# Attention with spread softmax sums: where in a step VectorE adds, inverts and sends them

## The chip, the cores and the metric

The kernel runs on one core of a Trainium2 chip. The metric is the time of one execution on the device in microseconds (us); the median of nine runs of the kernel before is 2945.12 us. A core has TensorE (PE: matmuls; its weight loads are listed as PEld), VectorE (DVE), ScalarE (ACT), GpSimd (POOL) and SyncE (SP, which here only issues DMAs). Each engine works through its own queue in order and waits on semaphores for the others.

## The reference

Two layers on 4 images of 32x32 tokens with 384 channels. The change lies in the first part of the first layer, an attention of 12 heads of 32 channels per image:

```python
attn = jax.nn.softmax(jnp.einsum('bhnd,bhmd->bhnm', q, k) * scale, axis=-1)
gp = gp_w.reshape(NH, GP_NUM, HD)
gidx = jnp.argmax(jnp.einsum('bhnd,hgd->bhng', q, gp), axis=-1)
gw = jax.nn.one_hot(gidx, GP_NUM, dtype=q.dtype)
q_mean = jnp.einsum('bhng,bhnd->bhgd', gw, q) / gw.sum(axis=2)[..., None]
qmw_t = jnp.einsum('bhgd,bhnd->bhgn', q_mean, k)
_, tidx = jax.lax.top_k(qmw_t, TOPK)
...
col = mask.sum(axis=2)
final = row[..., :, None] * col[..., None, :]
attn = attn * final
attn = attn / (attn.sum(axis=2, keepdims=True) + 1e-08)
out = jnp.einsum('bhnm,bhmd->bhnd', attn, v)
out = out.transpose(0, 2, 1, 3).reshape(B, H, W, NH * HD)
return out @ proj_w.T
```

The first sum of the softmax goes over the keys m; the second normalization goes over the queries n (axis 2), per key. So each exponential is multiplied by an inverse that belongs to its query, and the sum of these products over the queries gives a factor that belongs to its key. After the attention come a mixture of four experts, and a second layer with a local attention and a feed-forward part.

## The kernel before

**Tiles.** For each of 48 heads (4 images of 12; `NHEAD`), the scores stand with the keys on the 128 partitions and the 1024 queries along the row. A head has eight such tiles of 128 keys, taken two at a time in four *pairs* (`PAIRS`, u = 0 to 3). One pair is one *step* of the loop; there are 192 steps and a few more to drain (L860 and on). All engines' work of the attention stands in the order in which this loop issues it (the schedule of these engines is written by hand).

**One step**, in the order of issue:
- `scores(u)` (L617): eight matmuls, into `ps_s`.
- with u = 0, `gather` of the head before (L656 to L660): ScalarE copies the finished sums `ps_z` to `zr`; a DMA on SyncE's queue writes them to a row in DRAM (`z_row`), and a second one reads that row back as `zz`, with eight queries on each partition.
- `exps` (L627): ScalarE takes two exponentials of 128x1024 into the tiles `e`, of which there are 15.
- `out` of the pair seven steps back (`OUT`, L635 with `ps_o`): TensorE multiplies its `e` tiles by `wv`, the values with their factors. After a head's last pair, `keep` copies `ps_o` out (L706 to L715).
- with u = 1, `spread` of the head before (below).
- work of the preparation of the next image (norm, q, k, v, groups; `prepared`, among it DMAs that fetch input tiles, L199), top-k searches (`search`, `widen`), the projection of the image before and its routing, as far as a budget per step (`PACE`) and due times allow.
- `total(u)` (L635 with `ps_z`): TensorE sums the `e` tiles over the keys by a matmul with ones.
- in the first steps one DMA of zero fills for DRAM (L80, `room<-none`).
- `share` of the pair six steps back (`SHARE`, L683 to L693): VectorE multiplies the two `e` tiles by `rz` and by `inv` and sums each row in the same pass (L686, two passes), takes the reciprocal of the sums (L691) and multiplies the values by it (L693), which gives `wv`.
- `search`, the results of the step's other matmuls (`end`), `search` again; then, with u = 1, the next head's loads of `q4` and `k4` (L604, L605: eight DMAs on SyncE's queue).

**`spread`** (L665 to L680) takes the head's sums from `zz`: VectorE adds the two halves (L668, `zall`) and takes the inverse (L670, `rr`); a DMA writes it to a row in DRAM (`r_row`, L672), and a second one reads that row onto all 128 partitions as `rz` (L674, 512 KB). After an image's last head three small operations on VectorE follow (L678 to L680).

**The numbers of the steps.** Head m has its scores in steps 4m to 4m + 3. Its sums are gathered in step 4m + 4 and spread in step 4m + 5. Its four shares stand in steps 4m + 6 to 4m + 9, and its four `out` in steps 4m + 7 to 4m + 10. So step 4m + 5, in which head m is spread, also has the last share of head m - 1, and the first share of head m, which is the first to need `rz`, comes in the step after.

**A top-k search** (`topk`) alternates between ScalarE and VectorE: ScalarE counts the entries over a bound in one pass over 1024 (L360, L367, L404), VectorE moves the bound with two operations on one column (L371, L373) or picks the last entries (L380 to L401).

Of the kernel before, what the change touches and what calls it, by code (L numbers as in the profile page):

```python
# [153 lines left out]
def attention(net, outer, router, x, x1, unsafe, qkv_wT, gpT, proj_wT, proj_w, gate_w, gate_b):  # L154
# [15 lines left out]
    NHEAD = B * NH  # L170
# [9 lines left out]
    with ExitStack() as ctx:  # L180
# [120 lines left out]
        reached, heads, projected, valued = set(), [], set(), set()  # L301
# [415 lines left out]
        def value(b, t):  # L717
            im = images[b]
            if t % 2 == 0:
                im["v"].append(big.tile([P, 2, C], FP, name="v", tag="v", bufs=4))  # L720
            cost(2.0)
            ps = psum()
            linear(
                ps[:, : C + NE], lambda k: im["xnT"][:, k, t * P : (t + 1) * P],
                lambda k: wqkv[:, k, 2 * C :],
            )
            nc.scalar.copy(im["v"][t // 2][:, t % 2, :], ps[:, :C])
            nc.scalar.copy(im["x"][:, t, :], ps[:, C : C + NE])
            if t == NB - 1:
                valued.add(b)  # L730

        def residue(b, t):
            if late:
                o = late[0].tile([P, C], FP, name="o", tag="o", bufs=2)
            else:
                o = few.tile([P, C], FP, name="o", tag="o", bufs=1)
            residues[b, t] = o
            r = b * NTOK + t * P
            nc.sync.dma_start(out=o, in_=x[r : r + P, :])

        def project(b, t):
            im = images[b]
            r = b * NTOK + t * P
            if t == 0:
                im["o"] = few.tile([P, NB, NE], FP, name="gate_o", tag="gate_o", bufs=1)
                im["mv"] = few.tile([P, NB, 2], FP, name="mv", tag="mv")
            o = residues.pop((b, t))
            cost(2.0)
            ps = psum()
            linear(  # L750
                ps[:, : C + NE], lambda k: images[b]["q"][k][:, t * P : (t + 1) * P],
                lambda k: wproj[:, k, :],
            )
            projected.add((b, t))

            def add():
                nc.vector.tensor_tensor(o, o, ps[:, :C], ALU.add)
                nc.vector.tensor_copy(im["o"][:, t, :], ps[:, C : C + NE])
                st = few.tile([P, 6], FP, name="o_st", tag="o_st")
                nc.vector.bn_stats(st, o)  # L760
                nc.vector.bn_aggr(im["mv"][:, t, :], st)
                nc.sync.dma_start(out=x1[r : r + P, :], in_=o)

            ends.append(add)
# [42 lines left out]
        def prepared():  # L807

            nonlocal spent
            for i, unit in enumerate(pending):  # L810
                if unit is not None and (unit[1] is None or unit[1]()):
                    spent += unit[0]
                    pending[i] = next(preparing[i], None)
                    return True
            return False

        def search():

            for one in list(searching):
                if next(one, 0) == 0:  # L820
                    searching.remove(one)

        def widen(step):

            nonlocal begun
            if len(searching) < 2 and begun < len(tiles) and step >= begun * TURN - 9 and ready(*tiles[begun]):
                searching.append(topk(*tiles[begun]))
                begun += 1
                next(searching[-1])

        def begin(step):
            now[0] = step
            for f in others.pop(step, []):
                f()

        def end():
            while ends:
                ends.pop(0)()
# [21 lines left out]
        for step in range(STEPS + OUT + 2):  # L860
            n, u = divmod(step, PAIRS)
            if n < NHEAD:
                heads[n].scores(u)
            if u == 0 and 0 < n <= NHEAD:
                heads[n - 1].gather()
            if n < NHEAD:
                heads[n].exps()
            if 0 <= step - OUT < STEPS:
                heads[(step - OUT) // PAIRS].out((step - OUT) % PAIRS)
                if (step - OUT) % PAIRS == PAIRS - 1:  # L870
                    heads[(step - OUT) // PAIRS].keep()
            b, i = divmod(step, PAIRS * NH)
            goal = min(goal + (RAMP if step < 12 else PACE), spent + MOST)
            if u == 1 and 0 < n <= NHEAD:
                heads[n - 1].spread()
            begin(step)
            if step < 12:
                search()
                search()
            widen(step)  # L880
            o, t = i - OUT - 2, (i - OUT - 2) // 2
            if b and 0 <= o < 2 * NB and o % 2 == 0:
                project(b - 1, t)
            if b and 0 <= o + 1 < 2 * NB and o % 2:
                residue(b - 1, t + 1)
            if b and o > 2 * NB:
                next(routing[b - 1], None)
            if b < B:
                for t in {3: [0], 4: [1, 2], 5: [3], 6: [4], 7: [5, 6], 8: [7]}.get(i, []):
                    value(b, t)  # L890
            while spent < goal and prepared():
                pass
            if n < NHEAD:
                heads[n].total(u)
            if zeros and step >= 4:
                zeros.pop(0)()
            if 0 <= step - SHARE < STEPS:
                heads[(step - SHARE) // PAIRS].share((step - SHARE) % PAIRS)
            search()
            end()  # L900
            search()
            if u == 1 and n + 1 < NHEAD:
                heads.append(Head(n + 1))
# [1191 lines left out]
def metaformer_kernel(  # L2095
# [56 lines left out]
    with ExitStack() as outer:  # L2152
        router = routing(outer)
        eng = mybir.EngineType
        with tc.manual_schedule(engines={eng.PE, eng.DVE, eng.Activation, eng.SP}):
            left = attention(
                net, outer, router, x, x1, unsafe, qkv_wT, gpT, proj_wT, proj_w, gate_w, gate_b
            )
            done = experts(net, router, x1, x2, wup, wdown, left)
# [75 lines left out]
```

## Time and profile before

| | us |
|---|---|
| median of 9 runs | 2945.12 |
| lowest and highest run | 2934.11, 2950.93 |
| the profiled execution | 2950.63 |
| its span, first to last instruction | 2948.9 |
| TensorE busy in it | 2779.2 (94%) |
| VectorE busy | 1349.0 (46%) |
| ScalarE busy | 1215.7 (41%) |
| shares' passes on VectorE, L686, 384 of 1272 ns | 474.3 |
| exponentials on ScalarE, L627, 384 of 1110 ns | 408.0 |
| additions on VectorE, L668, 48 | first at 114.3, last at 1231.7 |

The busy times count an engine's own instructions; a matmul's end is modelled, so a busy TensorE need not be one at its peak. The profile's second part gives each engine's busy share in 40 equal slices of 73.7 us, as digits in tenths (9 is 90% or more). In the timeline, a row has its start, its duration, engine, line and operation, the tile written and the tiles read, and how many instructions are merged in it; in brackets stands the idle time of the engine just before and what ended it. In the list of waits, a row has the engine and line that waited, the releaser, the sum in us, the times and the longest. "SPq" is SyncE's queue, where the DMAs are issued. A row of windows has the stretch, its length, then busy time and count of PE, PEld, DVE, ACT and POOL, the granted clock of TensorE, the DMA engines' busy share and GB/s.

### The profile page before, as it was taken

The numbers are of one execution on the slowest core, as the hardware profiler recorded it, in microseconds if no ns is written. First come the engines' busy times: TensorE is split into PE (matmuls) and PEld (weight loads), VectorE is DVE, ScalarE is ACT, GpSimd is POOL, SyncE is SP. The second block draws the span as 40 slices with busy tenths as digits, with TensorE's granted clock in tenths as the row PEclk, the third lists the DMA queues.
The fourth block names the chain that finished last, engine by engine and source line by source line (L and its number), as shares of the span: only waits on it lengthen the run. The fifth ranks groups of instructions, "written<-read, shape, count | busy, mean of one in ns | idle before, by whom it ended". The sixth has DMA issues, their size and how long they took to land. (4 is left out here: it accounts for less than half of the span.)

```text
span 2948.9 us, 36681 instructions
## 1 busy us (share of the span) xinstructions
PE 2779.2 (94%) x13236; PEld 1474.5 (50%) x13236; DVE 1349.0 (46%) x3714; ACT 1215.7 (41%) x2023; POOL 395.2 (13%) x499
## 2 busy tenths in 40 slices
PE   6989999999989997699999999999999999999988
PEld 4323333333333332167777777777777754444433
DVE  1366777776766687633000001111111147777642
ACT  3777777777767776321121121121121122122135
POOL 1000000110021003114111112212211102100000
PEclk9999999999999998799999999999999999999988
DMA  5133334222322232355445455555555437544432
GB/s 102 43 99 93 94 93 128 74 58 68 97 54 58 66 101 63 113 204 194 172 183 190 171 195 207 195 210 214 191 214 211 144 134 238 188 154 161 143 104 87
DMA packets 216991, 405.91 MB, mean 138 GB/s; under 512 B 83504, under 2 KB 177904, under 8 KB 203744
## 3 DMA queue, kind: packets, MB, share of 16 engines
q1 hardware_dynamic: 186656, 190.77, 21.7%
q0 software_dynamic: 27152, 209.66, 20.7%
q10 hardware_dynamic: 2992, 3.03, 0.3%
q8 instruction: 107, 1.75, 0.3%
q14 instruction: 84, 0.69, 0.1%
HBM read 305.35 MB, written 49.99 MB: 120 GB/s over the span
## 5 line engine op out<-in xcount | busy, mean ns | idle before, releaser
L1611 ACT ACTIVATE h<-ps_h,up 128x256 f32<-128x256 f32 x420 | 199.0, 474 | 915.2 <-PE ps_h L1607 915.1
L1607 PE MATMUL ps_h<-xbT,up 128*128 128x256 f32 x2520 | 553.1, 380 | 2.6 <-ACT h L1611 1.8
L1624 PE MATMUL ps_y<-down,h 128*128 128x384 f32 x1680 | 554.9, 487 | 0.0
L1607 PEld LDWEIGHTS ps_h<-xbT,up 128*128 128x128 f32 x2520 | 479.5, 190 | 77.8 <-ACT h L1611 2.7
L686 DVE CUSTOM_DVE_ANT_0 e<-e,rz,inv 128x1024 f32<-128x1024 f32 x384 | 474.3, 1272 | 65.2 <-DMA rz<-r_row 65.2
L627 ACT ACTIVATE e<-ps_s,shift 128x1024 f32<-128x1024 f32 x384 | 408.0, 1110 | 118.0 <-PE ps_s L617 97.5
L1624 PEld LDWEIGHTS ps_y<-down,h 128*128 128x128 f32 x1680 | 317.4, 191 | 207.2 <-issue 1.5
L1629 DVE TENSOR_TENSOR y<-ps_y,down 128x384 f32<-128x384 f32 x70 | 39.0, 557 | 720.8 <-PE ps_y L1624 720.8
L635 PE MATMUL ps_z<-e,rt_ones 128*32 128x512 f32 x1536 | 266.2, 621 | 41.4 <-ACT e L627 41.4
L635 PE MATMUL ps_o<-e,wv 128*32 128x512 f32 x1536 | 220.9, 648 | 39.2 <-DVE wv L693 29.0
L617 PE MATMUL ps_s<-q,k 32*128 32x512 f32 x1536 | 230.3, 670 | 0.0
L713 POOL DMA_DIRECT2D q<-po x96 | 76.2, 873 | 994.0 <-DMA q<-po 544.5
L367 ACT ACTIVATE below<-tk_left,tk_bound 128x1024 bf16<-128x1024 f32 (+1 forms) x160 | 184.0, 1150 | 35.7 <-DVE tk_bound L373 16.4
L1735 PE MATMUL ps_a<-wa,xnT 128*128 128x486 f32 x384 | 166.2, 581 | 7.7 <-DVE attn L1745 6.0
L617 PEld LDWEIGHTS ps_s<-q,k 32*128 32x128 f32 x1536 | 61.9, 188 | 166.5 <-issue 165.7
L282 PE MATMUL ps_t<-xnT,wqkv 128*128 128x512 f32 x288 | 137.4, 618 | 7.2 <-ACT xnT L463 5.1
L635 PEld LDWEIGHTS ps_z<-e,rt_ones 128*32 128x32 f32 x1536 | 42.6, 110 | 190.8 <-ACT e L627 115.0
L635 PEld LDWEIGHTS ps_o<-e,wv 128*32 128x32 f32 x1536 | 31.3, 111 | 198.4 <-issue 77.2
L1735 PEld LDWEIGHTS ps_a<-wa,xnT 128*128 128x128 f32 x384 | 71.3, 191 | 91.9 <-issue 84.3
L1837 PE MATMUL ps_y<-band,v 128*32 128x194 f32 (+2 forms) x960 | 102.7, 517 | 7.4 <-DMA band<-room 7.2
L1576 DVE SCALAR_TENSOR_TENSOR x<-yt,weight,x 128x384 f32<-128x384 f32 x38 | 23.5, 619 | 185.7 <-DMA x<-x 185.0
L1490 POOL DMA_INDIRECT yt<-yg,index x64 | 66.0, 1032 | 302.5 <-DVE x L1576 140.5
(342 smaller groups left out, 2860.1 us busy)
## 6 DMA issues: line engine op xcount, KB each, us to landing
band<-room SPq DMA_DIRECT2D x32, 1560.0 KB
rz<-r_row SPq DMA_DIRECT2D x48, 512.0 KB
yg<-y SPq DMA_DIRECT2D x70, 192.0 KB
q<-q SPq DMA_DIRECT2D x192, 64.0 KB
k<-k SPq DMA_DIRECT2D x192, 64.0 KB
room<-none SPq DMA_DIRECT2D x64, 192.0 KB
x<-x SPq DMA_DIRECT2D x38, 192.0 KB
o<-in_x_dram SPq DMA_DIRECT2D x33, 192.0 KB
```

The costliest lines, as they stand in the source:

```text
L282: nc.tensor.matmul(ps, lhsT=lhsT(k), rhs=rhs(k), start=k == 0, stop=k == KC - 1)
L367: nc.scalar.activation(junk[:n], left[:n], AF.Sign, bias=bound[:n], accum_out=over[:n])
L617: nc.tensor.matmul(ps[:, half * 512 : half * 512 + 512], lhsT=self.k4[r, u * P : (u + 1) * P], rhs=self.q4[r, :], start=True, stop=True,)
L627: nc.scalar.activation(e, ps, AF.Exp, bias=shift, scale=QK_SCALE)
L635: nc.tensor.matmul(ps[r : r + 32, :], lhsT=lhsT(odd), rhs=self.es[2 * u + odd][:, half * 512 : half * 512 + 512], start=u == 0, stop=u == ...
L686: nc.vector.tensor_tensor_reduce(self.es[m], self.es[m], self.rz, 1.0, self.im["inv"][:, m, self.h : self.h + 1], ALU.mult, ALU.add, self. ...
L713: nc.gpsimd.dma_start(out=there, in_=po[r : r + 32, :], accum_op=ALU.add)
L1607: nc.tensor.matmul(ps, lhsT=up[:, o : o + P], rhs=xbT[:, k, :], start=k == 0, stop=k == KC - 1,)
L1611: nc.scalar.activation(h, ps, AF.Gelu, bias=up[:, KC * HID + f : KC * HID + f + 1])
L1624: nc.tensor.matmul(ps, lhsT=hs[f][:, t * P : (t + 1) * P], rhs=down[:, f * C : (f + 1) * C], start=f == 0, stop=f == NF - 1,)
L1735: nc.tensor.matmul(pa[:, hh, :HW_], lhsT=xnT[:, k, :], rhs=wa[:, k, hh * HW_ : (hh + 1) * HW_], start=k == 0, stop=k == KC - 1,)
L1837: nc.tensor.matmul(ys[c][32 * n : 32 * n + 32, lo - 512 * half : hi - 512 * half], lhsT=vs[b, t][:, h * HD : (h + 1) * HD], rhs=bands[b, t ...
```

## The change

`spread` is called later in the step: behind the shares that the step gives VectorE, instead of ahead of the step's preparations. The function itself stays as it is, and so does everything else.

```diff
             goal = min(goal + (RAMP if step < 12 else PACE), spent + MOST)
-            if u == 1 and 0 < n <= NHEAD:
-                heads[n - 1].spread()
             begin(step)
...
             if 0 <= step - SHARE < STEPS:
                 heads[(step - SHARE) // PAIRS].share((step - SHARE) % PAIRS)
+            if u == 1 and 0 < n <= NHEAD:
+                heads[n - 1].spread()
             search()
             end()
             search()
```

On VectorE's queue, the addition and the inverse of head m move behind the last share of head m - 1, and behind whatever else of the step's preparations VectorE has. On SyncE's queue, the issues of `r_row` and `rz` move behind what the preparations and the zero fills of that step issue there.

## The prediction, made before the changed kernel ran

> **What bounds the kernel now.** I read the page's slices first, then the waits of the attention stage alone (110 to 1260 us), then the timeline head by head, SyncE's queue among it.
>
> ```profile
> span 2948.9 us, 36681 instructions
> PE   6989999999989997699999999999999999999988
> DVE  1366777776766687633000001111111147777642
> ```
>
> TensorE (PE) is busy nearly everywhere. The change touches slices 2 to 17, the attention: there TensorE sets the pace, and VectorE (DVE) is 60 to 80% busy. What follows (experts, second layer) starts when the attention ends, and a delay of TensorE in the attention is a delay of the end.
>
> ```profile
> DVE e L686 <- DMA rz<-r_row: 65.2, 31, 6.1
> DVE zall L668 <- DMA zz<-z_row: 60.2, 27, 9.4
> PE ps_o L635 <- DVE wv L693: 29.0, 13, 6.5
> SPq L199 <- ACT xn L492: 14.9, 4, 5.2
> ```
>
> (us in all, times, longest.) VectorE waits twice per head: 27 of 48 times for the sums (zz), ahead of the addition, and 31 times for the spread inverse (rz), ahead of the head's first share. TensorE waits directly for a share's product only 13 times. Head 41 in the timeline shows the chain:
>
> ```profile
> 1097.28 0.17 DVE L668 TENSOR_TENSOR zall<-zz 128x8 f32<-128x8 f32 x1
> 1097.60 1.23 DVE L686 CUSTOM_DVE_ANT_0 e<-e,rz,inv 128x1024 f32<-128x1024 f32 x1
> 1097.71 0.32 SPq L672 DMA_DIRECT2D r_row<-rr  x1
> 1099.11 0.32 SPq L674 DMA_DIRECT2D rz<-r_row  x1
> 1100.35 0.23 DVE L693 TENSOR_TENSOR wv<-v,d 128x64 f32<-128x64 f32 x1
> ...
> 1103.25 1.28 DVE L686 CUSTOM_DVE_ANT_0 e<-e,rz,inv 128x1024 f32<-128x1024 f32 x1 [1.54 <-DMA rz<-r_row]
> ...
> 1106.05 0.23 DVE L693 TENSOR_TENSOR wv<-v,d 128x64 f32<-128x64 f32 x1
> ...
> 1106.52 1.06 PE L635 MATMUL ps_o<-e,wv 128*32 128x512 f32 x8
> ```
>
> Addition 1097.28; the share of the head before it, 1097.60 to 1100.58; the inverse goes out at 1097.71, comes back by 1103.25; the own first share ends at 1106.28, and TensorE takes it 0.24 us later. Addition to first share is 6.0 us, and VectorE waits within it.
>
> **The change, part by part.** Nothing is added or removed: addition (0.17 us) and inverse (0.20) of 48 heads, with two DMA issues each, move behind one share of VectorE: two passes of 1.28, two reads of 0.08, reciprocal 0.17, product 0.23, together 3.0 us from first start to last end (2.9 to 3.06 over the heads). The order of both programs' instructions shows it for 47 heads (head 0 has no share before it, only two top-k steps of 0.15); TensorE, ScalarE and GpSimd keep theirs.
>
> *Delay of the inverse.* If VectorE waited g for the sums, the share now runs inside that wait: the addition comes d = max(0, 3.0 - g) later. In 21 heads g is under 0.15 (d = 3.0), in 19 between, in 8 (4, 5, 10, 13, 17, 23, 27, 45) at least 3, where d = 0. In a few heads small operations stand between too (heads 18 and 30: 0.6; 26: 2.5). The transfers behind it, 1.4 us to r_row's landing and 4.0 to rz's (medians), move by d. If VectorE already waited for rz (31 heads), the first share starts d later; else d less the time by which rz was early. Over 48 heads these shifts add up to 77 us.
>
> *What hides it.* TensorE needs the product only at ps_o two steps later. The slack from the end of the product to that matmul, read per head, has a median of 2.8 us. Cover lacking is the difference: heads 0 1.0, 7 0.2, 8 0.3, 11 0.3, 14 0.4, 19 2.2, 30 0.7, 38 1.5, 39 0.1, 40 2.1, 41 2.6 (2.86 against 0.24), 43 3.0 (3.1 against 0.15), and in the tail 46 0.3 and 47 1.2, where every step waits for the last: 16 us. In the other heads the whole shift is covered.
>
> *ScalarE's queue.* Its top-k passes wait for VectorE operations behind the share, and the exponentials of the next step queue behind them; TensorE's sums (ps_z) wait for these. In head 8 VectorE runs from the share at 311.04 to L400 at 322.16 without a gap, ScalarE's L404 waits 0.94 for it, and TensorE then 2.76 for an exponential: the shift of 2.9 comes through, 2 us beyond the 0.3 above. Heads 7 and 38 give 1.2 and 0.6 in the same way: 4 us in all.
>
> *SyncE's queue.* The inverse's two DMAs are moved past what the step issues otherwise: zero fills of 192 KB, which wait for nothing, and once a fetch of input tiles (L199), in head 15's step:
>
> ```profile
> 466.70 0.32 SPq L672 DMA_DIRECT2D r_row<-rr  x1
> 468.24 0.32 SPq L674 DMA_DIRECT2D rz<-r_row  x1
> 473.85 0.38 SPq L199 DMA_DIRECT2D xt<-in_x_dram  x1
> ```
>
> That fetch stands from 468.6 to 473.85 waiting for ScalarE to have read the old tile. It will now stand ahead of r_row, which can go at about 474.9 (0.4 for the fetch, 0.54 for a zero fill). Right behind such a fetch the transfers are slow; head 17 has that order now:
>
> ```profile
> 522.03 0.38 SPq L199 DMA_DIRECT2D xt<-in_x_dram  x1
> 523.11 0.56 SPq L672 DMA_DIRECT2D r_row<-rr  x1
> 527.54 0.33 SPq L674 DMA_DIRECT2D rz<-r_row  x1
> 532.00 1.28 DVE L686 CUSTOM_DVE_ANT_0 e<-e,rz,inv 128x1024 f32<-128x1024 f32 x1 [6.14 <-DMA rz<-r_row]
> ```
>
> So r_row takes 4.4 and rz 4.4 instead of 1.5 and 3.6; rz lands at 483.8, the product comes 2.95 later at 486.7, and its matmul, at 479.07 now, waits 7.6 us (with the usual 1.4 and 4.0, 4.2 us). The next head's q and k loads, eight DMAs behind rz, shift by d too; in head 21 they are issued by 625 and used after 636, which covers 3 us. A later addition also holds r_row's SyncE place longer; stores of x1 stand behind it in both orders.
>
> *Gain.* VectorE's last share no longer waits for the sums, so what follows it in the step is earlier by min(3.0, g). TensorE profits where it waits for that: head 32, whose L404 waits 1.06, so 1.1 us. In the tail TensorE waits 6.48 (head 45) and 4.53 (head 47) for this very share, but its next product waits for rz (4.95 and 1.66), which comes no sooner: nothing.
>
> *Given back.* After a stall VectorE and ScalarE have caught up, and later waits in the same step shrink (41: 1.74 at the next product; 0, 7, 14, 43 in smaller ones): 5.5 us.
>
> *Clock.* TensorE's granted clock falls after some poor stretches:
>
> ```profile
> 1110.00:1115.00 5.00, 3.00 (x16) 0.60 (x16) 4.24 (x15) 4.77 (x7) 0.06 (x1) 1.00 0.14 21
> 1120.00:1125.00 5.00, 3.25 (x12) 0.53 (x12) 4.66 (x24) 2.13 (x3) 0.00 (x0) 0.66 0.02 1
> ```
>
> (The clock is the third column from the end.) A wait of 3.56 at 1112.0 leaves it at 1.00; after one of 1.74 at 1120.2 it is 0.66 of 5 us, 1.7 us lost, and while it is low eight ps_o matmuls take 1.92 us instead of 1.07. The seven new stalls over 1.4 us (8, 15, 19, 38, 40, 41, 43) can each cost 1.7 us or nothing: 0 to 12, and I take a third, 4, since both cases stand in these rows and part of the time TensorE has no work to lose.
>
> The sum: 16 + 4 + 7.6 - 1.1 - 5.5 + 4 = 25 us, on a profiled execution of 2950.6 (span 2948.9); that is 5.5 above the runs' median of 2945.1, so 2970 for the median.
>
> Two rules of the Trainium skill, which the sum does without. "DMA: Bandwidth & Descriptors", section Rules for kernel authors, speaks against the change: issue a DMA early, compute, and wait for it late. The trace agrees where slack is small (head 41), and not where the share fits into the wait for the sums (head 5, g = 3.5); taken without exceptions it would make the whole 77 us a loss. "TensorE: Matmul & The Clock Gate", Part 1, has the clock halved after an idle window of about 3.4 us; by it only head 15's stall would count, some 1.7 us instead of my 4 and 23 instead of 25; the rows above show 0.66 after shorter waits.
>
> **The rivals.**
> - *Covered.* The shifts stay in the slack, and the fetch has passed before r_row is ready. Slack of 2.8 against shifts of at most 3.6 speaks for it; the tail (1.5) less 1.1 gives 2945 to 2948. Against: slack under 0.3 in heads 40, 41 and 43, where TensorE already waits, and the fetch's wait ends at a ScalarE instruction that the change doesn't make earlier.
> - *Faster.* The 60.2 us of waiting for sums are filled with shares, and TensorE's two waits of 6.48 and 4.53 in the tail go: 2945 - 11 = 2934. It decides if rz, not the share, is early enough by 3 us in heads 45 and 47. Against: both of their first shares wait for rz now.
> - *VectorE becomes the bound.* Waits for rz rise by 3.0 in 31 heads (93 us) and waits for sums fall by under 60; where top-k work is dense the shift doesn't fade within the head. With half of the 77 us through, and head 15: 2945 + 46 = 2991.
>
> **How the numbers follow.** Forecast (2951 to 2984) 0.60, covered 0.15, faster 0.11, VectorE bound 0.14. The range of 2946 to 2990 reaches up to the sum with nothing given back and the full clock loss (25 + 5.5 + 8 = 38.5, so 2984) and a little into the third rival, and down past the sum with the short fetch, no clock loss and twice as much given back (25 - 3.4 - 4 - 5.5 = 12, so 2957) to the covered case. 0.2% (6 us) is about what a measurement of this kernel tells from no change: faster 0.11, same 0.15, slower 0.74.
>
> **What would show it.** In the changed profile: waits of L668 for zz nearly gone (about 10 us, most of it head 45), waits of L686 for rz above 130 us; a TensorE wait of 4 to 8 us at ps_o in head 15's second step, near 480; new waits of 2 to 3 us at ps_o in heads 38 to 43; the stages after the attention unchanged. Wrong, if TensorE's idle time before 1260 us doesn't grow, or if the waits for rz stay near 65.

## The result, and the profile after

| | before | changed |
|---|---|---|
| median, us (runs) | 2942.85 (31) | 2979.58 (10) |
| lowest and highest run | 2931.59, 2954.22 | 2972.32, 2988.47 |
| the profiled execution | 2950.63 | 2972.37 |
| its span | 2948.9 | 2970.3 |

The changed kernel is slower by a ratio of 1.0125, 95% interval [1.0109, 1.0141]: 36.7 us between the medians, where 25 were forecast. The two profiled executions lie only 21.7 us apart, because that of before is 8 us above its median and that of the changed kernel 7 us below its own; the readings of the traces below are to be taken with that.

The page of the changed kernel (span; busy share in 40 slices; then two groups with busy time and mean, and the idle time before them with what ended it):

```profile
span 2970.3 us, 36688 instructions
...
PE   6879998999989997689999999999999998999988
...
DVE  1366676667867676633000001111111146777742
...
L686 DVE CUSTOM_DVE_ANT_0 e<-e,rz,inv 128x1024 f32<-128x1024 f32 x384 | 475.4, 1275 | 169.4 <-DMA rz<-r_row 169.4
...
L617 PE MATMUL ps_s<-q,k 32*128 32x512 f32 x1536 | 230.8, 662 | 7.2 <-DMA k<-k 7.2
```

The shares' passes cost what they cost (1275 ns against 1272), so no work was added. What grew stands behind the second bar. The list of waits of the attention, with the columns of before:

```profile
DVE e L686 <- DMA rz<-r_row: 169.4, 43, 11.1
...
ACT below L367 <- DVE tk_bound L373: 51.9, 27, 5.7
...
PE ps_z L635 <- ACT e L627: 38.1, 35, 3.7
PE ps_o L635 <- DVE tk_parts L371: 22.8, 12, 4.0
PE ps_o L635 <- DVE wv L693: 18.8, 9, 9.2
...
PE ps_o L635 <- DVE tk_parts L377: 8.2, 2, 7.2
...
PE ps_s L617 <- DMA k<-k: 7.2, 2, 3.7
...
DVE zall L668 <- DMA zz<-z_row: 3.1, 5, 0.9
```

VectorE's 60.2 us of waits for the sums are down to 3.1; its waits for the inverse went from 65.2 us in 31 heads to 169.4 in 43. The share that stood in the first kind of wait now runs there, and the wait stands ahead of the next share, longer. Three releasers at ps_o are one thing: L371 and L377 are the small VectorE operations next behind the product L693, and the matmul starts 0.14 us after the product's end.

Where TensorE lost the time is read by adding up its waits from 110 us to the last `out` matmul, by the tile that waits and the releasing engine:

| TensorE waits, us | before | changed |
|---|---|---|
| ps_o, for VectorE | 39.1 | 52.5 |
| ps_z, for ScalarE's exponentials | 38.7 | 38.1 |
| ps_s, for the loads of k | 0 | 7.2 |
| ps_t (preparations, top-k), for ScalarE and VectorE | 16.5 | 18.3 |
| sum | 94.3 | 116.1 |
| TensorE busy in the same stretch | 1046.6 | 1049.6 |
| end of the last `out` | 1251.1 | 1275.9 |

The attention ends 24.8 us later: 21.8 of waits and 3.0 of busy time for the same matmuls. The stages behind it take 1113.6 us (experts, from their first matmul at L1607 to the last; 1118.2 before) and 577.6 (from there to the end, the second layer; 576.5): as forecast, the change adds nothing there.

Three places show how. Head 41, whose chain was shown of before, in the timeline:

```profile
1115.77 0.16 DVE L668 TENSOR_TENSOR zall<-zz 128x8 f32<-128x8 f32 x1
...
1116.19 0.32 SPq L672 DMA_DIRECT2D r_row<-rr  x1
1117.59 0.32 SPq L674 DMA_DIRECT2D rz<-r_row  x1
...
1121.92 1.28 DVE L686 CUSTOM_DVE_ANT_0 e<-e,rz,inv 128x1024 f32<-128x1024 f32 x1 [4.68 <-DMA rz<-r_row]
...
1124.73 0.23 DVE L693 TENSOR_TENSOR wv<-v,d 128x64 f32<-128x64 f32 x1
...
1125.10 1.30 PE L635 MATMUL ps_o<-e,wv 128*32 128x512 f32 x8 [2.69 <-DVE tk_parts L371]
```

Addition to first share is 6.15 us, as before (5.97); but the share of the head before is over, and VectorE waits 4.68 of it instead of 1.54. TensorE waits 2.69 us more; 2.6 were forecast for this head.

Head 15's step has the queue that was forecast:

```profile
481.23 0.38 SPq L199 DMA_DIRECT2D xt<-in_x_dram  x1
...
482.29 0.57 SPq L672 DMA_DIRECT2D r_row<-rr  x1
486.75 0.33 SPq L674 DMA_DIRECT2D rz<-r_row  x1
490.65 1.28 DVE L686 CUSTOM_DVE_ANT_0 e<-e,rz,inv 128x1024 f32<-128x1024 f32 x1 [11.08 <-DMA rz<-r_row]
...
493.75 1.94 PE L635 MATMUL ps_o<-e,wv 128*32 128x512 f32 x8 [7.24 <-DVE tk_parts L377]
```

The inverse was ready at about 475.2 (addition 474.81) and went out at 482.29, behind a fetch that waits for ScalarE; r_row took 4.4 us, rz 3.9, and TensorE waits 7.24 (forecast 7.6).

The third place was not in the forecast. In head 44's step the loads of the next head's q and k, which stand behind rz on SyncE's queue, land too late for the scores:

```profile
1210.45 1.38 PE L617 MATMUL ps_s<-q,k 32*128 32x512 f32 x2 [3.42 <-DMA k<-k]
1215.56 2.04 PE L617 MATMUL ps_s<-q,k 32*128 32x512 f32 x2 [3.73 <-DMA k<-k]
```

These are the whole 7.2 us at ps_s; before, the scores never waited for a load. The queues of the kernel before, and then of the changed one, at this place (the last load of each, and GpSimd's first fetch of expert weights):

```profile
1175.51 0.63 SPq L605 DMA_DIRECT2D k<-k  x1
1176.57 1.03 POOL L1524 DMA_INDIRECT up<-in_wup_dram,rows_w_first  x1 [0.30 <-issue]
```

```profile
1198.18 1.03 POOL L1524 DMA_INDIRECT up<-in_wup_dram,rows_w_first  x1 [2.70 <-PE ps_t L416]
...
1200.50 0.96 SPq L605 DMA_DIRECT2D k<-k  x1
```

Before, all eight loads were out when the weights' fetch began; now half of them come behind it. By the trace the last k load lands 2.9 us after its issue in the first case and 14.9 us in the second, at 1215.42, and the matmul starts at 1215.56. So the loads were not late by the shift alone: the shift put them behind the weights' fetch. The 14 profiles of this document agree in the main. In eight of them the last k load is issued ahead of the fetch, and no score waits; in three it is issued 2.3 us behind it, and two scores wait 7.2 to 7.5 us in all; in three it is 0.6 to 1.0 us behind, with a wait of 3.5 us in one of them and none in two.

### The profile page after: what moved, and what is told of

The parts are those of the page before. It is cut to its first block, busy times and chain, and to the rows that moved or that the text cites. A ratio compares the mean times of both kernels' runs of the same rounds, so it can differ in the third digit from the quotient of the medians.

```text
span 2970.3 us, 36688 instructions
## 1 busy us (share of the span) xinstructions
PE 2781.9 (94%) x13236; PEld 1477.1 (50%) x13236; DVE 1346.6 (45%) x3714; ACT 1214.3 (41%) x2023; POOL 395.3 (13%) x499
## 5 line engine op out<-in xcount | busy, mean ns | idle before, releaser
L1607 PE MATMUL ps_h<-xbT,up 128*128 128x256 f32 x2520 | 553.5, 380 | 2.6 <-ACT h L1611 1.8
L686 DVE CUSTOM_DVE_ANT_0 e<-e,rz,inv 128x1024 f32<-128x1024 f32 x384 | 475.4, 1275 | 169.4 <-DMA rz<-r_row 169.4
L1607 PEld LDWEIGHTS ps_h<-xbT,up 128*128 128x128 f32 x2520 | 479.8, 191 | 77.9 <-ACT h L1611 2.7
L635 PE MATMUL ps_z<-e,rt_ones 128*32 128x512 f32 x1536 | 274.1, 635 | 41.8 <-ACT e L627 41.8
```

The lines of the kernel that those rows point to most:

```text
L635: nc.tensor.matmul(ps[r : r + 32, :], lhsT=lhsT(odd), rhs=self.es[2 * u + odd][:, half * 512 : half * 512 + 512], start=u == 0, stop=u == ...
L686: nc.vector.tensor_tensor_reduce(self.es[m], self.es[m], self.rz, 1.0, self.im["inv"][:, m, self.h : self.h + 1], ALU.mult, ALU.add, self. ...
L1607: nc.tensor.matmul(ps, lhsT=up[:, o : o + P], rhs=xbT[:, k, :], start=k == 0, stop=k == KC - 1,)
```

## The experiments

The kernels ran in three groups of four, each group on one chip together with the kernel before, and they are compared within their group only. The kernel before took 2973.0 us (median) with the first four kernels, 2973.1 with the next four and 2944.4 with the last four. Slack is the time from the end of a first share's product to its matmul.

**Which heads cost the time.** Three kernels make only some heads late. The 14 listed ones are those for which the forecast's sum had a term, apart from head 15: 0, 7, 8, 11, 14, 19, 30, 38 to 41, 43, 46 and 47.

```diff
+    LATE = {0, 7, 8, 11, 14, 19, 30, 38, 39, 40, 41, 43, 46, 47}
...
-            if u == 1 and 0 < n <= NHEAD:
+            if u == 1 and 0 < n <= NHEAD and n - 1 not in LATE:
                 heads[n - 1].spread()
...
                 heads[(step - SHARE) // PAIRS].share((step - SHARE) % PAIRS)
+            if u == 1 and 0 < n <= NHEAD and n - 1 in LATE:
+                heads[n - 1].spread()
```

> Only the 14 heads that the prediction lists as lacking cover (0, 7, 8, 11, 14, 19, 30, 38, 39, 40, 41, 43, 46, 47) are spread behind the share; the other 34 stay ahead of it. My theory (cost only where the slack behind the first share is under the shift): these carry nearly all of the change but for the fetch, 20 to 30 us over before (the prediction's sum without the fetch and with its clock term is 17). Rival (slack differs from execution to execution, so every late head costs alike): 14 of 48 heads of 36.7, about 11 us.

Measured: ratio 1.0080 [1.0061, 1.0100], medians 22.3 us apart. The 14 heads carry most of the price, twice what they would if every head cost the same.

The other 33 heads late, all but head 15, whose shift the forecast called covered:

> The complement: only the 33 heads that the prediction calls covered are spread behind the share, without head 15. My theory: 0 to 5 us over before. Rival (every late head costs alike): 33 of 48 of 36.7, about 25 us; a rival that VectorE's lost time itself is the cost says the same.

Measured: 1.0037 [1.0020, 1.0055], medians 9.8 us apart. A miss for both theories, and a real price: even the lower bound, 0.2% or 6 us, is above what the forecast allowed these heads. Its timeline has new waits of TensorE in heads 1, 3, 21 and 26, for these products:

```profile
153.51 1.07 PE L636 MATMUL ps_o<-e,wv 128*32 128x512 f32 x8 [0.41 <-DVE col L433]
...
204.45 1.06 PE L636 MATMUL ps_o<-e,wv 128*32 128x512 f32 x8 [0.90 <-DVE tk_parts L378]
...
647.09 1.07 PE L636 MATMUL ps_o<-e,wv 128*32 128x512 f32 x8 [0.77 <-DVE tk_parts L372]
...
768.31 1.07 PE L636 MATMUL ps_o<-e,wv 128*32 128x512 f32 x8 [1.34 <-DVE tk_parts L372]
```

Together 3.4 us, in heads whose slack before was 3.28, 2.23, 4.35 and 3.80. In head 1 the shift was larger than forecast. A top-k operation that waits for a pass of ScalarE stands between the place where the addition was (140.01 in the kernel before) and the share:

```profile
141.08 0.16 DVE L407 SCALAR_TENSOR_TENSOR topped<-tk_parts,tk_over 128x1 f32<-128x1 f32 x1 [1.23 <-ACT tk_left L405]
...
144.09 0.16 DVE L669 TENSOR_TENSOR zall<-zz 128x8 f32<-128x8 f32 x1
```

Counted from the gathering, the addition comes 4.3 us later there, not 3.0. All waits at ps_o sum up to 48.3 us in this execution, 9 more than in either profile of the kernel before (39.1, and 39.3 in the second one below). Part of it is in the tail, at heads 44 and 45:

```profile
1200.44 1.06 PE L636 MATMUL ps_o<-e,wv 128*32 128x512 f32 x8 [2.69 <-DVE wv L694]
1227.40 1.94 PE L636 MATMUL ps_o<-e,wv 128*32 128x512 f32 x8 [12.57 <-DVE wv L694]
```

These 15.3 us stand against 9.7 and 13.0 at the same two heads in the profiles of the kernel before. One execution doesn't show how much of this each of the others has.

Head 15 alone late:

> Only head 15 is spread behind the share, the one whose two DMAs then stand behind the fetch of input tiles on SyncE's queue. My theory: about 7 us over before at once, some of it given back later: 3 to 8 us in all. Rival (the fetch's place doesn't matter, the share does): under 1 us.

Measured: 1.0021 [1.0007, 1.0036], medians 4.0 us apart. Its TensorE waits 7.46 us for the product; part of that is regained behind it. The three parts add up, 22.3 + 9.8 + 4.0 = 36.1 us, to what the whole change costs (36.7). That speaks for a price made up by head. It doesn't prove it: each part is known to 4 to 6 us only, and the 7.2 us of waits for k are in none of the three profiles.

**The fetch.** The changed kernel, with a step's fetch of input tiles issued behind the inverse's two DMAs:

```diff
-        def fetch(b, half, tag="xt"):
+        held, holding = [], [False]
+
+        def fetch(b, half, tag="xt", now=True):
+            if not now:
+                held.append((b, half, tag))
+                return
...
-                    fetch(b, 1)
+                    fetch(b, 1, now=not holding[0])
...
+            holding[0] = u == 1 and 0 < n <= NHEAD
...
                 heads[n - 1].spread()
+            while held:
+                fetch(*held.pop(0))
```

> The changed kernel, but a fetch of input tiles that falls into a step with a spread is issued behind the spread's two DMAs. My theory: the changed kernel's 36.7 us less the fetch's share, 29 to 34 over before, and no wait of 11 us for rz near 487. Rival (the fetch is hidden or given back): 36.7 as it was.

Measured: 1.0099 [1.0078, 1.0120], medians 27.7 us apart, a little under what the theory gave. In the timeline of head 15 the order is turned, and TensorE doesn't wait there:

```profile
477.93 0.33 SPq L677 DMA_DIRECT2D r_row<-rr  x1
479.34 0.33 SPq L679 DMA_DIRECT2D rz<-r_row  x1
483.24 1.28 DVE L691 CUSTOM_DVE_ANT_0 e<-e,rz,inv 128x1024 f32<-128x1024 f32 x1 [1.04 <-DMA rz<-r_row]
483.86 0.38 SPq L204 DMA_DIRECT2D xt<-in_x_dram  x1
```

r_row lands in 1.4 us instead of 4.4, and VectorE waits 1.04 instead of 11.08. By the times alone the gain over the changed kernel is not certain (the intervals touch, and the chips differ); that the order on the queue makes head 15's wait is shown by this timeline and by the experiment on head 15 alone.

**How late matters.** The same spread at two other places: behind the preparations and zero fills but still ahead of the share (`spread` moved up past the `share` call), and between the share's two passes.

> The spread of all heads stands behind the step's preparations and zero fills, as in the changed kernel, but still ahead of the share. My theory (the share's 3.0 us and head 15's fetch are the price, the preparations are not): the fetch's 3 to 8 us and little else, so 3 to 9 over before. Rival (standing behind the preparations and zero fills on both queues costs by itself): 15 us or more.

Measured: 1.0010 [0.9994, 1.0026], medians 4.1 us apart, the size of head 15's part. So it is the share, 3.0 us of VectorE, that costs the rest, not the preparations.

```diff
-            def share(self, u):
+            def share(self, u, between=None):
...
                 for m in (2 * u, 2 * u + 1):
                     nc.vector.tensor_tensor_reduce(...)
+                    if between and m == 2 * u:
+                        between()
...
```

> As the changed kernel, but the addition and the inverse stand between the share's two passes: the shift is 1.3 us less the wait instead of 3.0. My theory (a threshold: only what exceeds the slack costs): by the rows of before 3 us beyond slack instead of 17, with the fetch's 4 and about 2 for heads near the threshold, 6 to 13 over before. Rival (cost proportional to the whole shift in TensorE's time, plus the fetch): 20 of 72 of the other 33 us, 9, with the fetch 13; a rival that leaving the wait for the sums unfilled is what counts says 25 or more.

Measured: 1.0042 [1.0027, 1.0057], medians 12.0 us apart. Between 6 and 13, as the theory had it, but a price in proportion to the delay (13) is not excluded by this run. The 25 us of the last rival are.

**Heads that wait long for their sums.** Nine heads late in which VectorE had waited 2.96 us or more for the sums, so that the share should fit into that wait: `LATE = {4, 5, 9, 10, 13, 17, 23, 27, 45}`.

> Only the nine heads in which VectorE waits 2.9 us or more for the sums in the trace of before (4, 5, 9, 10, 13, 17, 23, 27, 45) are spread behind the share, which then fits into the wait. My theory: no shift of rz and no wait of TensorE for it: -3 to +3 us. The rival that filling VectorE's wait makes the kernel faster says -5 to -11; the rival that each late head costs alike says +7.

Measured: 1.0022 [1.0005, 1.0039], medians 6.3 us apart; nothing is gained, and the theory missed too. The size is that of the rival in which each late head costs alike (7). The list of waits shows what became of the room:

```profile
DVE e L687 <- DMA rz<-r_row: 75.6, 31, 8.1
DVE zall L669 <- DMA zz<-z_row: 30.6, 27, 3.4
```

Half of the waiting for sums is filled, and the waits for rz grow by 10 us: VectorE is done with the share sooner and waits later. For TensorE that is no gain: the product needs rz, rz needs the sums, and these land when they did. Counted from the end of the gathering of the sums (L656), the product ends at 13.64, 12.62, 12.74 and 14.28 us in heads 5, 9, 10 and 13, and at 13.64, 12.72, 12.56 and 14.29 in the kernel before (its second profile, below). Against the same profile it is late in head 4, by 1.2 us, and in head 23, 15.00 against 12.26, where addition to landing of rz took 8.32 us instead of 5.86. Head 4 has slack left (1.43); at head 23 TensorE waits 1.51. Where the 6.3 us [1.5 to 11.6 by the ratio] come from isn't seen in these rows and stays open; the profiled execution, 2971.05 us, is itself 8 us under this kernel's median.

**How stable the slack is.** The kernel before once more, with a profile:

> The kernel before, a second profiled execution. My theory for the 33 heads called covered, if they cost something (slack is not the same in each execution): the slack behind the first share differs between the two executions by 1 us or more in at least a third of the heads. Rival (slack is fixed by the program's order): it differs by under 0.5 us in nearly all, and the covered heads' cost has another cause.

One profiled execution, 2976.64 us. The slack differs from the first profile by 1 us or more in 10 of 48 heads, by 0.5 in 17, between what theory and rival had. Heads 3 and 21 have 0.87 and 2.65 instead of 2.23 and 4.35. The forecast's sum over uncovered shifts, done with these rows, gives 13.7 us for the listed heads and 2.3 for the others, instead of 16.0 and 0.1. So a few heads look covered in one profile that in another execution are not; 2.3 of the 9.8 us are explained by it and the rest is not.

**Loads ahead of the inverse.** The changed kernel, with the eight loads of q4 and k4 issued ahead of the inverse's DMAs:

```diff
+            if u == 1 and n + 1 < NHEAD:
+                heads.append(Head(n + 1))
             if u == 1 and 0 < n <= NHEAD:
                 heads[n - 1].spread()
             search()
             end()
             search()
-            if u == 1 and n + 1 < NHEAD:
-                heads.append(Head(n + 1))
```

> The changed kernel, with the next head's loads of q4 and k4 (eight DMAs) issued just ahead of the spread's two DMAs instead of behind them; on the engines nothing moves. Theory (TensorE's waits of 7.2 us for k in head 44's step come from loads that stand behind a late rz): these two waits are gone, and with the rest unchanged the kernel is 27 to 34 us above the kernel before. Rival (that stretch had other waits of this size in the kernel before, and they come back): the waits for k are gone too, but the time stays 35 to 40 us above. Third: eight loads ahead of r_row make rz later in every head, and the time is 40 us or more above.

Measured: 1.0318 [1.0293, 1.0342], medians 97.0 us apart. The waits for k are gone, and the third outcome came true, at twice the size it named. In the timeline of head 4:

```profile
226.52 0.60 SPq L604 DMA_DIRECT2D q<-q  x1
227.16 0.62 SPq L605 DMA_DIRECT2D k<-k  x1
227.89 0.53 SPq L672 DMA_DIRECT2D r_row<-rr  x1
229.51 0.33 SPq L674 DMA_DIRECT2D rz<-r_row  x1
...
233.02 1.28 DVE L686 CUSTOM_DVE_ANT_0 e<-e,rz,inv 128x1024 f32<-128x1024 f32 x1 [4.06 <-DMA rz<-r_row]
```

Each load takes about 0.64 us of SyncE's queue, and the inverse (ready at 222.5) stands behind them. Over the heads the median from the inverse's end to its issue is 1.98 us instead of 0.03 (15 heads keep 0.03, one has 12.7), and the median from addition to landing 7.99 instead of 5.96. In this kernel TensorE's waits at ps_o sum up to 102.6 us, and its busy time in the attention to 1072.9, since the granted clock is 0.92 there (0.95 in the changed kernel). What the late loads of k cost by themselves stays open: this order paid for them with something dearer.

**ScalarE's route.** Top-k operations that stand on VectorE behind the wait for rz hold up ScalarE's next pass. The first of the step's two search calls is put ahead of the share, in each head's first share step, in three kernels: the changed one, the 33 covered heads late, and the kernel before as control.

```diff
+            if u == 2:
+                search()
             if 0 <= step - SHARE < STEPS:
                 heads[(step - SHARE) // PAIRS].share((step - SHARE) % PAIRS)
...
-            search()
+            if u != 2:
+                search()
             end()
             search()
```

> The changed kernel, with the first of the two top-k search calls issued ahead of the share, in each head's first share step alone, so that VectorE does the search's small operations before it waits for rz. Theory (part of the cost comes over ScalarE: top-k operations stand behind VectorE's wait for rz, ScalarE's next pass waits for them, 52 us against 15 before, and the exponentials queue behind that pass): ScalarE's waits for tk_bound fall below 30 us and the time is 20 to 31 us above the kernel before. Rival (the cost comes through the products alone, and a search ahead of the share makes them 0.3 us or more later): 34 to 45 us above, whatever ScalarE's waits do.

Measured: 1.0086 [1.0061, 1.0111], medians 28.8 us apart. Its waits:

```profile
DVE tk_parts L371 <- ACT below L367: 93.0, 41, 5.9
DVE e L686 <- DMA rz<-r_row: 91.0, 31, 7.1
...
ACT below L367 <- DVE tk_bound L373: 18.5, 14, 5.7
```

ScalarE's waits for the bound fall from 51.9 to 18.5 us, as the theory had it: they did come from operations queued behind rz. The time is within the theory's range, but its interval touches that of the changed kernel, and TensorE's waits don't show the way: those at ps_z are 38.1 us in the changed kernel's profile and 36.2 in this one, those at ps_o 52.5 and 58.4.

> The 33 heads late that the forecast called covered (which gave +9.8 us), with the same move of the search in all heads' first share steps. Theory (the covered heads cost something over ScalarE): 0 to 6 us above the kernel before, once the control (the kernel before with the same move) is taken off. Rival (slack differs from execution to execution, or each shift costs its share through the product): 8 to 13 above the control.

Measured: 1.0018 [1.0001, 1.0036]; less the control 0.0021, some 6 us, against 0.0037 for the same heads without the move. That is between the two, and the intervals overlap: inconclusive.

> The control: the kernel before, with the first search call ahead of the share in each head's first share step. VectorE waits for rz in 31 heads of it (65 us), so the search mostly runs inside a wait; in the others the product comes 0.3 us later, up to 2.5 in the seven heads where the search picks its last entries. Theory: within 6 us of the kernel before, 2967 to 2979 on this chip; faster by 3 us or more if ScalarE's 15 us of waits for tk_bound were on the path; slower by 6 or more if the products were.

Measured: 0.9997 [0.9975, 1.0019], no difference. (The chip was another than the expectation took it for; the kernel before has 2944.4 us there.) So the move by itself is neutral, within 6 to 7 us. In its profile VectorE's waits for rz fall from 65.2 to 18.5 us and those of L371 for ScalarE's pass rise from 27.2 to 78.5: the waiting of an engine that is not the bound changes its place, and nothing follows from it. No version beats the kernel before.

## Why the prediction was right, and where not

**Direction and mechanism: right.** One share of 3.0 us between the sums' landing and the addition makes rz late, VectorE waits for it at the next share, and TensorE pays where the slack is smaller than the delay. Shown by the 14 heads against the other 33 (22.3 against 9.8 us, or 1.6 us per head against 0.3), by the spread ahead of the share (4.1 us) and by the timelines of heads 15 and 41. Of the signs that were named, the waits for rz (above 130; 169.4), those for the sums (about 10; 3.1) and the unchanged stages came true; 22 heads now have a slack under 0.3 us, 8 before. TensorE's wait in head 15 came at 493.75 rather than near 480, since the fetch itself left 7.4 us later than before.

**The rivals.** Covered and Faster fall by the ratio; Faster also by the nine wide waits, where filling the waits for the sums gained nothing. VectorE as the bound (+46) was not reached: the ratio's interval is 32 to 41 us, and VectorE is busy 800.9 us of the attention's 1166. But the forecast's 25 lies outside that interval too, and 36.7 is nearer to 46. Of that rival the waits for rz came true (93 us more; measured 104), and of the 77 us of shifts 0.42 came through by the runs, where it had half and the forecast's sum without head 15 less than a quarter.

**Term by term**, with the forecast's own terms beside what the traces of this pair and the runs show:

| term | forecast | measured |
|---|---|---|
| listed heads (with their ScalarE, gain, regain and clock terms) | 17.4 | 22.3 by runs |
| other heads | 0 | 9.8 by runs |
| head 15 | 7.6 | 4.0 by runs; its wait 7.24 |
| TensorE at ps_o, all | 17.0 net | 13.4 in the pair of traces |
| at ps_z, by ScalarE's queue | 4 | -0.6 in the pair of traces |
| at ps_s, loads of k | 0 | 7.2 in the pair of traces |
| clock | 4 | 3.0 in the pair of traces |

(17.0 is 16 + 7.6 - 1.1 - 5.5; 17.4 is 25 less 7.6.) The trace's own pair gives 24.8 us by the end of the attention, the forecast's 25 almost to the point; but two terms that were wrong, ScalarE's and the loads', offset each other there, so that agreement is luck. Against the medians the sum is 12 us short. (The first three rows divide the cost by heads, the last four by what TensorE waited for; the two don't add up together.)

**The step that failed** is "in the other heads the whole shift is covered". Those heads cost 9.8 us [6 to 16 by the ratio's bounds]. The forecast took slack as a threshold, read from one execution, and followed each head's delay to the next matmul at ps_o and no further. The runs show three things it left out. The slack of a head moves by 1 us or more from one execution to the next in 10 of 48 heads, so a shift just under it is covered in one execution and not in another. The new waits in heads 3, 21 and 26 are of this kind: counted from the gathering, TensorE came to these matmuls 1.3 to 1.4 us sooner than in the first profile of before. Next, the shift was more than a share in head 1, where an operation that waits for ScalarE stands in between (4.3 us against a slack of 3.28). And other work stands behind rz, the top-k operations on VectorE and the next loads on SyncE. The loads were considered and passed over with "which covers 3 us", read at head 21; at head 44 the shift put them behind the fetch of expert weights, and 3 us were not enough. How the 9.8 us divide is not settled: the second profile accounts for 2.3, four heads' waits in another for 3.4, heads 44 and 45 there for 2 to 6, the search kernels leave ScalarE's share uncertain, and the loads could not be moved without a larger loss. Nine of these heads, for which the forecast had next to no shift, cost 6.3 us in a run of their own, and that stays unexplained.

**The price rises faster than the delay.** Four kernels have the same spread at increasing delay: 0 behind the preparations (and the fetch), 1.3 us in the middle of the share, 3.0 behind it, and about 5 behind the loads too. They cost 4, 12, 37 and 97 us, each against the kernel before on its own chip. Each further us, in 48 heads, cost 6, then 15, then 30 us. In their profiles 10, 13, 22 and 32 heads have a slack under 0.3 us (8 in the kernel before), so slack is used up in more heads. The fourth delay is a median, uneven over the heads, and the lower clock is part of its price. At the last step it is 0.6 us of time per us of delay and head.

The "DMA: Bandwidth & Descriptors" page of the Trainium skill, section Rules for kernel authors, asks for a DMA to be issued early and waited for late. These runs agree, and price it: the forecast's shifts add up to 77 us and cost 37.

## What to carry to other kernels

A step moved behind other work is paid for where its result is consumed. Read the slack there in more than one execution, count a place whose slack is within 1 us of the shift as partly exposed, and follow everything that queues behind the late result on every engine and queue, DMA issues included: eight loads ahead of a small DMA cost more here than the whole change. Filling a wait on an engine that is not the bound gains nothing unless a result comes sooner by it: 57 us less waiting for the sums stood against 104 us more waiting for rz.

## What the hardware showed that was not expected

A 4 KB write issued right behind a fetch of input tiles takes 4.4 us to land (head 15 of the changed kernel) and 1.4 when issued ahead of it; the order on the queue made 3 us.

On the two chips where the kernel before takes 2973 us there are waits that the traces of the chips at 2943 and 2944 us don't have. In the second profile of the kernel before, while GpSimd issues scatters:

```profile
595.75 1.11 ACT L627 ACTIVATE e<-ps_s,shift 128x1024 f32<-128x1024 f32 x1 [6.84 <-remote]
...
602.87 0.56 DVE L548 TENSOR_REDUCE g_max<-ps_t 128x8 f32<-128x384 f32 x1 [9.97 <-remote]
```

From 593 to 603 us TensorE is busy for 2.2 us, VectorE for 0.1 and ScalarE for 2.8; waits with this releaser ("remote": one that the profile doesn't name) sum up to 60 us over the program, 28 of them behind the attention. Their cause isn't shown. All eight profiles taken on these two chips have them, 34 to 65 us in each, the kernel before among them.

TensorE's clock: in the changed kernel all four waits at ps_o of 3.5 us and more (3.53, 4.01, 7.24, 9.23) are followed by eight matmuls in 1.93 or 1.94 us instead of 1.06. After shorter ones, 1.0 to 3.02 us, it is mixed, from 1.06 to 1.94. "TensorE: Matmul & The Clock Gate" of the Trainium skill, Part 1, names an idle window of about 3.4 us for the halving: the long waits of this kernel agree. Not all of the other kernels' do: with the search ahead of the share a wait of 3.83 us is followed by 1.06, and with the loads ahead of the inverse one of 4.01 by 1.34. Whether the clock was already low at the short ones, these rows alone don't tell.
